# Layer 1's 128-column products as two 64-column tiles

## The chip, the core and the metric

The program runs on one core of one Trainium2 chip. A core has a matrix engine (TensorE, PE in the profile; its weight loads are shown apart as PEld), a vector engine (VectorE, DVE), a scalar engine (ScalarE, ACT), a general one (GpSimd, POOL), queues that issue transfers (SyncE, SP, is the one used most here), an on-chip memory of 128 partitions, and accumulators (PSUM) that TensorE writes and ACT and DVE read. The metric is the device time of one execution in microseconds (us); lower is better.

## What is computed

Two attention layers on an image of 128 rows x 256 positions x 256 channels, each after a group normalisation and with a residual sum. Layer 1 is the one that matters here:

```python
qkv = x2 @ w_in.T + b_in                       # x2: rows x 256 x 256
q, k, v = jnp.split(qkv, 3, axis=-1)
...
scores = jnp.einsum('bhid,bhjd->bhij', q, k) / jnp.sqrt(D)     # 4 heads of D = 64
keep = jnp.abs(i - j) <= band                                  # band = 16
scores = jnp.where(keep, scores, -jnp.inf)
attn = jax.nn.softmax(scores, axis=-1)
out = jnp.einsum('bhij,bhjd->bhid', attn, v)
...
y = out @ w_out.T + b_out
```

and then `x = x + y`. Everything is in 32-bit floats. Layer 0 is of the same build with 8 heads of 32, full attention, and a gate.

## The kernel before

Layer 0 runs over the 128 rows first, writes its result to memory, and gathers the statistics of the second normalisation. Layer 1 then runs over pairs of rows, 64 of them. In layer 1 the order of all engines and of SP is written out by hand (a manual schedule), so every engine does its instructions in the order of the program text.

The loop (i from 0 to 62) does in this order on TensorE: the scores of rows 2i and 2i+1 (tile `1sim`, line 1076, tiles of 64 rows x 64 columns); the weighted values of pair i-1 (`1av`, line 1117, 64 x 64) and their sums of weights (`1zs`, line 1129, 64 x 32); then the "stretch": the q and k products of pair i+1 and the output product of pair i-2 (`p1q`, `p1k`, `p1o`, all recorded at line 577); then the values of the next pair (`p1v`, line 1055, 128 rows x 64 columns, two column halves side by side).

A q, k or output product of a pair of rows is a 256 x 256 matrix times 2 x 256 columns. Class `Summed` does it with seven 128 x 128 products instead of eight, from sums of quarters of the weights and of rows (tiles `1ts`, `1att`, made on POOL). The seven go in the order 2, 1, 5, 6, 7, 4, 3, and at each number the three streams q, k, output take turns (`in_turn`). After each product its accumulator is read (`take`): q and k by ACT (lines 675, 677) or DVE (684, 690, 694), the output always by DVE (671 and the same three). The next product of the same stream waits for that. Each product is handed to TensorE by one helper, which cuts it into column tiles of a given width:

```python
def in_columns(out, lhsT, rhs, width, **flags):
    for c0 in range(0, P, width):
        cols = slice(c0, c0 + width)
        nc.tensor.matmul(out[cols], lhsT=lhsT[:, cols], rhs=rhs, **flags)
```

Layer 0 uses it with a width of 32 (`B`). In layer 1 the width is 128 (`P`): in `Summed.WIDTH`, and in `project`, the output product of the last six rows, which have no stretch left (`1po`). The names are P = 128, D1 = 64, B = 32.

Beside the stretch run these chains. DVE makes the reciprocals of the sums (`1z` to `1rz`, lines 1141 and 1154), in three parts between its takes; SP sends them out to memory and back, spread over partitions (`rz_far`, `1near`, lines 1162 and 1166); DVE multiplies (`1at`, line 1186), which frees the accumulator of `1av` for the next pair. In the tail the same spreading is done by a product (`1near`, line 1177, 128 x 128). A 32-bit product shows as two records (passes) in the profile, each with its weight load.

Of the kernel before, what the change touches and what calls it, by code (L numbers as in the profile page):

```python
# [15 lines left out]
P = 128  # L16
# [5 lines left out]
H1, D1 = 4, 64  # L22
# [17 lines left out]
def conv_preact_kernel(  # L40
# [35 lines left out]
    def proj_bank(name):  # L76
        return bank("proj", name)
# [67 lines left out]
    w_out_t = const.tile([P, 2, C], F32, name="w_out_t")  # L145
# [427 lines left out]
# [6 lines that stand above are left out]
    class Seven:  # L579

        WIDTH = B

# [9 lines left out]
        def product(self, n, two=None, first=False):  # L592
# [7 lines left out]
            if not self.by_token:  # L600
                in_columns(out, weights, moving, self.WIDTH, start=first, **flags)
                return
            for t2 in range(2):
                cols = slice(t2 * P, (t2 + 1) * P)
                in_columns(out[:, cols], moving[:, cols], weights, self.WIDTH, start=first and t2 == 0, **flags)

# [47 lines left out]

    class Summed(Seven):

        WIDTH = P

# [50 lines left out]
    def one_by_one(w, at, name, done, width):  # L711

        ps = proj_bank(name)
        done(ps)
        for m in range(2):
            for kt in range(2):
                in_columns(
                    ps[:, m, :], w[:, kt, m * P : (m + 1) * P], at[:, kt, :], width,
                    start=(kt == 0), stop=(kt == 1),
                )  # L720
                yield
# [10 lines left out]
    with ExitStack() as both:  # L732
# [20 lines left out]
        with ExitStack() as lay0:  # L753
            row = lay0.enter_context(tc.tile_pool(name="row0", bufs=2))
            att = lay0.enter_context(tc.tile_pool(name="att0", bufs=2))
            st, hd, outs = {}, {}, {}
# [224 lines left out]
        with ExitStack() as lay:  # L981
# [3 lines left out]
            st, hd, outs = {s: {} for s in range(S)}, {}, {}  # L985
# [38 lines left out]
            def project(s):  # L1024

                if s < 0:
                    return iter(())
                return one_by_one(w_out_t, st[s]["at"], f"1po{s}", lambda ps: st[s].update(po=ps), P)

            ats, ats_t, outputs, last_ots = {}, {}, {}, {}  # L1030

# [221 lines left out]
            with tc.manual_schedule(engines={  # L1253
# [12 lines left out]
                for i in range(last):  # L1266
                    s = 2 * i
# [22 lines left out]
                def all_of(s):  # L1290
                    for _ in project(s):
                        pass
# [240 lines left out]
```

## Time and profile before

| | |
|---|---|
| median of 3 runs | 3150.04 us (3149.86 to 3153.88) |
| the profiled execution: its time, and its span from the first to the last instruction | 3153.9 us, 3152.1 us |
| layer 1's loop and tail | from about 2071 us to the end |
| TensorE busy from 2071 to 3110 us | 1034.31 of 1039.00 us |
| DVE, ACT, POOL busy in the same stretch | 667.78, 553.72, 740.75 us |
| p1q, p1k, p1o: records, mean | 896, 896, 854; about 380 ns |
| p1v: records, mean | 4096; 274 ns |

How to read it: "128*64" behind a tile's name is the tile of the array (rows*columns) that a product uses, "128x256" is what it writes. The mean of a matmul record runs from its start to its modelled end, and passes overlap, so the step from one start to the next is the measure of what a product costs TensorE, not the mean.

### The profile page before, as it was taken

How to read it: one execution, taken by the hardware profiler on the slowest of the kernel's cores; microseconds unless marked ns; L12 is line 12 of the kernel's file. 1: busy time of each engine (PE TensorE's matmuls, PEld its weight loads, DVE VectorE, ACT ScalarE, POOL GpSimd, SP SyncE). 2: the span in 40 equal slices, each digit the busy share in tenths (PEclk: the TensorE clock that was granted, in tenths of full speed). 3: DMA queues.
4: the chain of work that ended last, by engine and by line, in shares of the span. 5: the costliest groups of instructions: out<-in, count | busy, mean ns of one | idle time of the engine just before them, and what ended most of it. 6: DMA issues, size and time to landing. Idle time of an engine off the chain costs nothing.

```text
span 3152.1 us, 128861 instructions
## 1 busy us (share of the span) xinstructions
PE 3075.5 (98%) x57467; PEld 2114.1 (67%) x57467; DVE 2544.5 (81%) x4140; ACT 1870.0 (59%) x4064; POOL 1622.5 (51%) x1651
## 2 busy tenths in 40 slices
PE   6889999999999999999999999999999999999997
PEld 4556666666666666665666666568888888888886
DVE  4669999999999999999999999956666666666665
ACT  4666666666666666666666666645555555555553
POOL 3034444444444444444444544357777777776774
PEclk9989999999999999999999999999999999999999
DMA  9941111111111111111111111114444444444443
GB/s 374 424 121 43 43 43 36 43 36 43 36 39 40 40 40 36 43 36 43 36 42 37 36 43 36 36 35 98 93 103 96 102 96 97 103 99 100 93 99 70
DMA packets 357266, 245.08 MB, mean 78 GB/s; under 512 B 276072, under 2 KB 342112, under 8 KB 350560
## 3 DMA queue, kind: packets, MB, share of 16 engines
q1 hardware_dynamic: 355808, 234.39, 27.3%
q8 instruction: 453, 7.42, 1.0%
q0 software_dynamic: 752, 2.36, 0.2%
q14 instruction: 109, 0.89, 0.1%
q10 hardware_dynamic: 144, 0.00, 0.0%
HBM read 169.09 MB, written 67.62 MB: 75 GB/s over the span
## 4 chain that ended last, share of the span: by engine, by line
PE 91%; DMA 5%; DVE 2%; ACT 1%; issue 0%; POOL 0%; SPq 0%; DVEq 0%; POOLq 0%; ACTq 0%
PE sim L794 8%; PE po L577 7%; PE p1v L1055 7%; PE bv L826 7%; PE av L826 7%; PE p1q L577 6%; PE p1o L577 6%; PE pv L577 6%; PE pq L577 6%; PE p1k L577 6%; PE pk L577 5%; PE pg L577 5%; DMA pr<-in_L_conv_pair_repr_dram 4%; PE zs L840 4%; PE 1sim L1076 3%; PE 1av L1117 3%
## 5 line engine op out<-in xcount | busy, mean ns | idle before, releaser
L807 ACT ACTIVATE ex<-sim 128x512 f32<-128x512 f32 x1024 | 547.6, 605 | 422.2 <-PE sim L794 422.2
L816 DVE TENSOR_TENSOR both<-ex 128x512 f32<-128x512 f32 x512 | 487.8, 991 | 71.2 <-ACT ex L807 71.0
L856 DVE RECIPROCAL d<-d 128x512 f32<-128x512 f32 x128 | 429.2, 3353 | 4.4
L618 POOL TENSOR_TENSOR v<-v,twovg 128x256 f32<-128x256 f32 x64 | 78.3, 1223 | 544.4 <-ACT twovg L637 544.4
L577 PE MATMUL po<-at,out_sb 128*32 128x256 f32 x4096 | 291.5, 380 | 4.1 <-DVE at L874 4.1
L794 PE MATMUL sim<-q,k 32*64 32x256 f32 x8192 | 288.4, 387 | 1.2 <-ACT ex L807 1.2
L826 PE MATMUL bv<-bias_sb,v 128*32 128x256 f32 x4096 | 244.5, 379 | 0.7 <-DVE t L871 0.7
L826 PE MATMUL av<-ex,v 128*32 128x256 f32 x4096 | 244.5, 379 | 0.0
L1086 POOL TENSOR_TENSOR 1p<-1ex,seen 128x768 f32<-128x768 f32 x127 | 231.0, 1819 | 13.9 <-ACT 1ex L1084 13.9
L1055 PE MATMUL p1v<-w_in_t,1xn 128*64 128x128 f32 x4096 | 237.7, 274 | 0.3 <-POOL place L990 0.3
L794 PEld LDWEIGHTS sim<-q,k 32*64 32x64 f32 x8192 | 152.1, 131 | 126.9 <-issue 79.3
L1055 PEld LDWEIGHTS p1v<-w_in_t,1xn 128*64 128x64 f32 x4096 | 222.3, 137 | 21.5 <-PE p1k L577 20.2
L677 ACT ACTIVATE 1q<-p1q,bqk 128x256 f32<-128x256 f32 x192 | 91.1, 474 | 244.1 <-PE p1q L577 244.1
L1186 DVE TENSOR_TENSOR 1at<-1av,1near 128x512 f32<-128x512 f32 x128 | 82.5, 686 | 151.5 <-DMA 1near<-rz_far 129.0
L618 POOL TENSOR_TENSOR q<-q,twoqk 128x256 f32<-128x256 f32 x64 | 52.0, 812 | 292.4 <-ACT twoqk L637 292.4
L826 PEld LDWEIGHTS bv<-bias_sb,v 128*32 128x32 f32 x4096 | 133.2, 110 | 88.7 <-issue 1.1
L826 PEld LDWEIGHTS av<-ex,v 128*32 128x32 f32 x4096 | 133.2, 110 | 87.9 <-issue 0.4
L577 PEld LDWEIGHTS po<-at,out_sb 128*32 128x32 f32 x4096 | 131.0, 110 | 70.9 <-issue 4.5
L1093 POOL TENSOR_TENSOR 1zp<-1p 128x512 f32<-128x512 f32 x127 | 161.9, 1275 | 10.0
L568 POOL TENSOR_TENSOR 1ts<-1xn 128x256 f32<-128x256 f32 x64 | 47.0, 734 | 232.9 <-ACT 1xn L1016 232.9
L775 DVE TENSOR_SCALAR xn<-xt,mean,rstd 128x256 f32<-128x256 f32 x256 | 160.4, 666 | 0.0
L1062 ACT COPY 1v<-p1v 128x512 f32<-128x512 f32 x128 | 75.1, 587 | 135.1 <-PE p1v L1055 131.7
(300 smaller groups left out, 7687.6 us busy)
## 6 DMA issues: line engine op xcount, KB each, us to landing
pr<-in_L_conv_pair_repr_dram SPq DMA_DIRECT2D x32, 1024.0 KB
xs<-in_x_dram SPq DMA_DIRECT2D x16, 2048.0 KB
x<-o SPq DMA_DIRECT2D x64, 512.0 KB
yg<-x SPq DMA_DIRECT2D x64, 512.0 KB
out_dram<-1o SPq DMA_DIRECT2D x256, 128.0 KB
xg<-in_x_dram SPq DMA_DIRECT2D x252, 128.0 KB
1near<-rz_far SPq DMA_DIRECT2D x124, 256.0 KB
rz_far<-1rz SPq DMA_DIRECT2D x124, 4.0 KB
```

The lines of the kernel that those rows point to most:

```text
L577: nc.tensor.matmul(out[cols], lhsT=lhsT[:, cols], rhs=rhs, **flags)
L618: nc.gpsimd.tensor_tensor(self.to[:, 0], self.to[:, 0], two, ALU.add)
L775: nc.vector.tensor_scalar(xns[i][:, 2 * r + half, :], xt[:, half, :], mean0[:, half : half + 1], rstd0[:, half : half + 1], op0=ALU.subtra ...
L794: nc.tensor.matmul(sims[j][KB * c : KB * (c + 1), kt, :], lhsT=k[p0 : p0 + D0, 2 * r + half, k0 : k0 + KB], rhs=q[p0 : p0 + D0, 2 * r + ha ...
L807: nc.scalar.activation(ex[:, j], sims[j], AF.Exp, scale=1.0 / math.sqrt(D0))
L816: nc.vector.tensor_tensor(both[:, j : j + 2], ex[:, j : j + 2, 0, :], ex[:, j : j + 2, 1, :], ALU.add)
L826: nc.tensor.matmul(to[D0 * j : D0 * (j + 1), half, :], lhsT=v[:, 2 * r + half, c0 : c0 + D0], rhs=weights(4 * half + j, kt), start=(kt == ...
L840: nc.tensor.matmul(zs[D0 * j : D0 * (j + 1), half, :], lhsT=ones[:, 0:D0], rhs=both[:, j, :], start=True, stop=True,)
L856: nc.vector.reciprocal(d, d)
L1055: nc.tensor.matmul(ps[KB * half : KB * (half + 1), b, :], lhsT=xns[i][:, 2 * r + kt, KB * b : KB * (b + 1)], rhs=w_in_t[:, kt, 2 * C + P * ...
L1086: engine.tensor_tensor(p.rearrange("p j (r c) -> p (j r) c", c=WROW)[:, :, 0 : 2 * WSTEP] .rearrange("p r (t c) -> p r t c", c=WSTEP)[:, : ...
L1093: engine.tensor_tensor(zp, p[:, :, 0:R], p[:, :, R : 2 * R], ALU.add)
```

## The change

Two widths go from 128 to 64 columns. Every q, k and output product of layer 1, and the output products of the last six rows, are then issued as two products of 64 columns each on the two column halves of the array, with the same moving operand, into the two halves of the accumulator's partitions. Nothing else is edited.

```diff
     class Summed(Seven):
 
-        WIDTH = P
+        WIDTH = D1
...
             def project(s):
 
                 if s < 0:
                     return iter(())
-                return one_by_one(w_out_t, st[s]["at"], f"1po{s}", lambda ps: st[s].update(po=ps), P)
+                return one_by_one(w_out_t, st[s]["at"], f"1po{s}", lambda ps: st[s].update(po=ps), D1)
```

## The prediction

> **What bounds the kernel now.** I read the page first (busy time, the slices, the chain of waits), then the timeline of TensorE and of its weight loads in one iteration of layer 1's loop, then who waited for whom. From the page:
>
> ```profile
> PE 3075.5 (98%) x57467; PEld 2114.1 (67%) x57467; DVE 2544.5 (81%) x4140; ACT 1870.0 (59%) x4064; POOL 1622.5 (51%) x1651
> PE   6889999999999999999999999999999999999997
> PEclk9989999999999999999999999999999999999999
> PE 91%; DMA 5%; DVE 2%; ACT 1%; issue 0%; POOL 0%; SPq 0%; DVEq 0%; POOLq 0%; ACTq 0%
> ```
>
> TensorE is the bound, at full clock, and the chain that ended last lies on it for 91% of the span. Layer 1 is the part from about 2071 us. Its loop runs 63 times, usually in 16.37 us (start of the values p1v to start of the next: 2599.88 to 2616.25), so only a change in TensorE's spacing, or in what stops TensorE, can move the end. One iteration in the timeline of TensorE (columns: start us, us, engine, line, operation, tiles, tile shape, count):
>
> ```profile
> 2599.88 3.71 PE L1055 MATMUL p1v<-w_in_t,1xn 128*64 128x128 f32 x64
> 2604.96 1.41 PE L1117 MATMUL 1av<-1p,1v 64*64 64x80 f32 x63
> 2606.31 0.66 PE L1129 MATMUL 1zs<-1zp,place 64*32 64x256 f32 x16
> 2606.90 0.70 PE L577 MATMUL p1q<-1xn,w_in_t 128*128 128x256 f32 x2
> 2607.44 0.59 PE L577 MATMUL p1k<-1xn,w_in_t 128*128 128x256 f32 x2
> 2607.87 0.59 PE L577 MATMUL p1o<-1at,w_out_t 128*128 128x256 f32 x2
> ...
> 2611.32 0.59 PE L577 MATMUL p1k<-1ts,sums_1k 128*128 128x256 f32 x2
> 2611.75 0.64 PE L577 MATMUL p1o<-1att,sums_1o 128*128 128x256 f32 x2
> 2612.23 0.59 PE L577 MATMUL p1q<-1ts,sums_1q 128*128 128x256 f32 x2
> 2612.66 0.59 PE L577 MATMUL p1k<-1ts,sums_1k 128*128 128x256 f32 x2
> 2613.09 0.64 PE L577 MATMUL p1o<-1att,sums_1o 128*128 128x256 f32 x2
> 2613.57 0.59 PE L577 MATMUL p1q<-1ts,w_in_t 128*128 128x256 f32 x2
> ...
> 2615.72 0.59 PE L577 MATMUL p1o<-1at,sums_1o 128*128 128x256 f32 x2
> 2616.25 0.33 PE L1055 MATMUL p1v<-w_in_t,1xn 128*64 128x128 f32 x2
> ```
>
> Each product is two records (two passes), so the usual 0.43 from start to start is 0.216 us a pass; the durations 0.59 overlap. The reader is to see the four places where the step is longer than 0.43: p1q to p1k 0.54, two p1o to p1q 0.48, and p1o to p1v 0.53. These are all that a tile shape can change here.
>
> **What the Trainium skill says.** TensorEngine Tiling (Array Packing), Key Properties: a change of tiling mode drains TensorE, and different tiles work in parallel. The trace agrees: from the last pass's start plus its 0.216 us, p1v starts 0.093 us late (2615.941 + 0.216 to 2616.250, the records to the ns), p1q after zs 0.09, while stages of one shape follow each other with no gap (in layer 0, products bv to av, both 128*32: 32 passes in 1.73 us, four tiles together every 0.216). TensorE: Matmul & The Clock Gate, LDWEIGHTS: a load lasts its columns / 1.2 ns, so 107 ns for 128 columns, 53 for 64. The trace shows the part that isn't hidden after a drain: p1q's first step is 0.320 instead of 0.216 (+0.104), p1v's first step 0.160 instead of 0.109 (+0.051). Same page, the paragraph on step 1 (LDWEIGHTS): loads are pulled ahead of running matmuls. Here they are issued one pass ahead, except where a wait holds them.
>
> **The change part by part.**
>
> 1. The rate of the products. Each 128-column product becomes two 64-column ones side by side. No run here has 128*64 with 256 elements moving, so I bound it: below by layer 0's helper of the same line, four 128*32 tiles of 256 elements every 0.216 us, the same as the full tile, so no cost; above by the values, pairs of 128*64 with 128 moving at 0.109 us, which doubled is 0.218: 42 steps of 2 ns, 0.1 us per iteration. I take 0. Weight loads go from 42 to 84 per iteration; two loads of a pair start 6 ns apart and the first values pair shows both exposed by only 0.051 together, so they run at once.
>
> 2. p1o to p1v (and in the first stretch p1v to p1q): now one shape. The drain of 0.093 and the exposed load of 0.051 go: 0.144 x 63 = 9.1 us. What is late next there is the values' matmul rate itself: ACT's 1v copies and the scores wait for it, not the reverse (ACT 1v waited 131.7 us for p1v).
>
> 3. zs to p1q: still a change of shape (64*32 to 128*64), so the drain stays, but the exposed load is 64 columns: 0.104 - 0.051 = 0.053.
>
> 4. The two p1o stalls, 0.044 and 0.043. The weight load of p1o (2611.69, of the product that starts at 2611.75) waits for DVE's take of the product before, then for a second wait instruction of 0.076 us; from 2611.69 it needs 0.107 and has 0.06. With 64 columns it needs 0.053. But the first take (L671 at 2611.09) starts where DVE's reciprocal ends, a chain fixed by zs, not by the products. So part 3's 0.053 brings the product forward and the shorter load just follows: after this stall the gain is 0.053 in all, not 0.097. The second take is fixed by p1o's own end (DVE idle 0.40 before it), so there the stall of 0.043 goes, with some 3 ns to spare. Other loads that wait for ACT or DVE (p1q, p1o) have 0.01 to 0.03 us to spare now; they get 0.053 more.
>
> 5. New waits. Set side by side, the two programs have the same order on every engine, but many of ACT's and DVE's takes (four ACT and nine DVE per iteration) now wait for two semaphores: PE's, and that of an older piece of work on ACT or DVE, long done. On ACT, and for p1o on DVE, the older one is waited for first, by an instruction of its own that runs before PE is done: 0. For DVE's takes of q and k PE comes first: at most one instruction of 0.05 us (L1154's: 50 ns) after PE's end. Queued behind it are the takes of k and o, and their next products on PE. Mostly DVE is still in the operation before, which hides it; uncovered it costs up to 0.05 at two places, 0.1 per iteration. I take 0.
>
> Sum per iteration: 0.144 + 0.053 + 0.043 = 0.24 us, from 16.37 to 16.13. Over the loop (61 iterations have p1o): 63 x 0.197 + 61 x 0.043 = 15.0 us. The first stretch gains 0.2.
>
> 6. What takes some of it back. In 14 of 63 iterations 1av starts 0.06 to 0.58 us later than usual, because it waits for DVE's 1at, and this for the transfer:
>
> ```profile
> DVE 1at L1186 <- DMA 1near<-rz_far: 127.3, 53, 3.7
> POOL 1att L568 <- DVE 1at L1186: 28.0, 26, 1.8
> ```
>
> The chain zs, reciprocals, two transfers (6.3 to 8.4 us from the last reciprocal to 1at), 1at, 1av has a length that the change leaves alone: in those iterations the gain is 0. Four more have less than 0.07 us in hand (1at's end to 1av 0.15 to 0.21 us, where 0.145 is the least seen); the next has 0.36. Loss: 14 x 0.24 + about 0.8 = 4.2 us.
>
> 7. The tail. There the output product alternates with the 128*128 product 1near, of one shape until now. Three new changes of shape, 0.093 + 0.05 each, about 0.4 us; half of it may lie beside DVE's reciprocals. Taken in full.
>
> 15.0 + 0.2 - 4.2 - 0.4 = 10.6 us. The profiled execution (span 3152.1, its time 3153.9) would go to 3143.3; it was the longest of the runs shown, and I take the same gain off the median: 3150.04 - 10.6 = 3139.5.
>
> **Rivals.**
>
> The waits keep more. If the new DVE waits show (0.1 us per iteration, 6 us) or the transfers are late in twice as many iterations (4 us more), 4 to 6 us are left: about 3145.5. For it: the slack of many loads is only hundredths of a us. Against: every one of them is given 0.053.
>
> More than forecast. Where the transfers' lateness came from a coincidence with loads and stores that the shorter loop shifts, nothing is lost in part 6, and the first p1o stall goes too: 15.2 + 61 x 0.044 = 17.5, about 3133.
>
> The change doesn't do what it says: the 0.093 before p1v isn't a drain but a wait (the profile names p1k as its releaser, with 0.33 us of idle weight loads). Then only parts 3 and 4 are left, 15.2 - 9.1 - 2.4 for the late iterations = 3.7, about 3146. Against: p1k had ended 0.36 us before, and three different changes of shape show the same 0.09.
>
> Slower: the halves don't run together where the first of them is held by a semaphore. Nearly every product begins with a held load. If the second half only follows in the next pass, a product costs three passes for two, 0.216 more; it decides from 49 of the loop's 1309 products (10.6 / 0.216), and for all of them gives 3139.5 + 283 = 3422. Against: layer 0's 128*32 products also begin with held loads, and their four tiles start within 0.02 us.
>
> **How the numbers follow.** Forecast 0.55, own range 3135 to 3143; waits keep more 0.13; more than forecast 0.12; no drain 0.10; slower 0.10. The range 3132 to 3147 takes in all but the slower case and the edges. 0.2%, about what a measurement of this kernel can tell from no change, is 6.3 us: faster means below 3143.7. That is the forecast, the larger gain and some 0.05 of the two smaller gains: 0.72; within 0.18; slower 0.10.
>
> **What would show it.** Right: p1v starting 0.216 us after the last p1o pass with no step over 0.11 among its first pairs; p1q to p1k 0.48; one p1o step of 0.48 instead of two; the usual iteration 16.13; 1av late in some 16 to 20 iterations. Wrong: pairs spaced over 0.22, the 0.53 step before p1v still there, new gaps after DVE's takes L684, L690 or L694, or 1av late in most iterations.

## The result, and the profile after

| | before | changed |
|---|---|---|
| median | 3152.24 us (3149.86 to 3155.4, 8 runs) | 3143.48 us (3141.82 to 3144.71, 8 runs) |
| ratio to before, from all runs | | 0.9971, 95% interval 0.9961 to 0.9982 |
| profiled execution: time, span | 3153.9, 3152.1 us | 3144.71, 3142.9 us |
| usual iteration (median), from p1v to p1v | 16.371 us | 16.175 us |
| loop, first p1v to last p1v | 1042.36 us | 1032.08 us |

The change gained 8.8 us in the medians (0.28%); the forecast was 10.6. The whole gain of the profiled pair lies in the loop: 10.28 us there. Outside it the span lost 1.1 us: 0.15 in the tail's products and 0.9 after the last of them, a part that took 13.5 us before, 14.4 here and 13.9 in another profile of the changed kernel. From the page of the changed kernel, its busy times, its instruction queue (packets, MB, share) and its chain:

```profile
PE 3062.3 (97%) x60161; PEld 2030.7 (65%) x60161; DVE 2542.5 (81%) x4140; ACT 1869.8 (59%) x4064; POOL 1623.3 (52%) x1651
q8 instruction: 474, 7.77, 1.1%
PE 91%; DMA 5%; DVE 2%; ACT 1%; issue 0%; POOL 0%; SPq 0%; DVEq 0%; POOLq 0%; ACTq 0%
```

TensorE has 2694 more records (one more for each pass of a split product) and is still the bound: DVE, ACT and POOL are as busy as before, and the chain has the same shares. TensorE's own busy time shows 13 us less, but since its records overlap, the spacing is what to read. A usual iteration in the timeline of TensorE:

```profile
2611.32 3.69 PE L1055 MATMUL p1v<-w_in_t,1xn 128*64 128x128 f32 x64
...
2617.71 0.66 PE L1129 MATMUL 1zs<-1zp,place 64*32 64x256 f32 x16
2618.30 0.65 PE L577 MATMUL p1q<-1xn,w_in_t 128*64 128x256 f32 x4
2618.79 0.60 PE L577 MATMUL p1k<-1xn,w_in_t 128*64 128x256 f32 x4
...
2620.51 0.60 PE L577 MATMUL p1o<-1at,w_out_t 128*64 128x256 f32 x4
2620.95 0.65 PE L577 MATMUL p1q<-1ts,sums_1q 128*64 128x256 f32 x4
2621.39 0.63 PE L577 MATMUL p1k<-1ts,sums_1k 128*64 128x256 f32 x4
...
2623.12 0.65 PE L577 MATMUL p1o<-1att,sums_1o 128*64 128x256 f32 x4
2623.58 0.63 PE L577 MATMUL p1q<-1ts,sums_1q 128*64 128x256 f32 x4
2624.01 0.63 PE L577 MATMUL p1k<-1ts,sums_1k 128*64 128x256 f32 x4
2624.44 0.65 PE L577 MATMUL p1o<-1att,sums_1o 128*64 128x256 f32 x4
2624.90 0.63 PE L577 MATMUL p1q<-1ts,w_in_t 128*64 128x256 f32 x4
...
2627.06 0.63 PE L577 MATMUL p1o<-1at,sums_1o 128*64 128x256 f32 x4
2627.49 3.69 PE L1055 MATMUL p1v<-w_in_t,1xn 128*64 128x128 f32 x64
```

A product is four records now, two passes of two halves side by side, and its step is still 0.432. The reader is to see four things. The last p1o to p1v is 0.43: the step of 0.53 is gone, and with it the drain, the 0.093 us by which the first product of a new tile shape started late. The first p1q to p1k is 0.49 instead of 0.54. But both of the long p1o steps are still there, at 0.46 instead of 0.48; the forecast had one of them at nothing. And the p1q of 2620.95 takes 0.44: a small stall that the kernel before didn't have.

In the table below each entry is the median over the loop of the step beyond 0.432, in thousandths of a us, from the starts of single records. The products bear the number of their order (2, 1, 5, 6, 7, 4, 3) and the stream; "3o" is the step from the last p1o to p1v, and p1v is that whole stage, from its first start to the scores'. An "exposed" weight load, below, is one that no running product hides.

| | 2q | 5q | 6k | 6o | 7k | 7o | 3o | p1v, us |
|---|---|---|---|---|---|---|---|---|
| before | 104 | 0 | 0 | 43 | 0 | 42 | 93 | 3.644 |
| changed | 51 | 16 | 4 | 21 | 4 | 21 | 0 | 3.623 |

With 11 from 1av and zs these differences make up the 0.196.

### The profile page after: what moved, and what is told of

Same layout as the page of the kernel before. It is cut to its first block, busy times and chain, and to the rows that moved or that the text cites. A ratio compares the mean times of both kernels' runs of the same rounds, so it can differ in the third digit from the quotient of the medians.

```text
span 3142.9 us, 135072 instructions
## 1 busy us (share of the span) xinstructions
PE 3062.3 (97%) x60161; PEld 2030.7 (65%) x60161; DVE 2542.5 (81%) x4140; ACT 1869.8 (59%) x4064; POOL 1623.3 (52%) x1651
## 4 chain that ended last, share of the span: by engine, by line
PE 91%; DMA 5%; DVE 2%; ACT 1%; issue 0%; POOL 0%; SPq 0%; DVEq 0%; POOLq 0%; ACTq 0%
PE sim L794 8%; PE po L577 7%; PE av L826 7%; PE bv L826 7%; PE p1v L1055 7%; PE p1q L577 6%; PE p1o L577 6%; PE p1k L577 6%; PE pv L577 6%; PE pq L577 6%; PE pk L577 5%; PE pg L577 5%; DMA pr<-in_L_conv_pair_repr_dram 4%; PE zs L840 4%; PE 1sim L1076 3%; PE 1av L1117 3%
## 5 line engine op out<-in xcount | busy, mean ns | idle before, releaser
L1055 PEld LDWEIGHTS p1v<-w_in_t,1xn 128*64 128x64 f32 x4096 | 231.6, 137 | 6.0 <-POOL place L990 0.6
L334 DVE BATCH_NORM_STATS2 stats<-xs 128x6 f32<-128x128 f32 x512 | 100.3, 277 | 65.1 <-DMA xs<-in_x_dram 65.1
```

The source lines that it names most:

```text
L1055: nc.tensor.matmul(ps[KB * half : KB * (half + 1), b, :], lhsT=xns[i][:, 2 * r + kt, KB * b : KB * (b + 1)], rhs=w_in_t[:, kt, 2 * C + P * ...
```

## The experiments

Ten kernels ran in three groups, each compared with runs of the kernel before in its group (medians 3151.65 to 3151.76 us; 3152.24 beside the changed kernel). Times are medians. The table gives what the loop of each profile showed; "late 1av" counts the iterations in which 1av starts later than usual and what those iterations lost, "other" is what was lost beyond the usual iteration in any other way.

| kernel | median | ratio to before, 95% | usual iteration | late 1av | other | loop |
|---|---|---|---|---|---|---|
| before | | | 16.371 | 13: 3.9 us | 1.1 us | 1042.36 |
| changed | 3143.48 | 0.9971 (0.9961 to 0.9982) | 16.175 | 14: 4.0 | 3.1 | 1032.08 |
| changed, once more | 3142.93 | 0.9972 (0.9962 to 0.9983) | 16.178 | 14: 3.2 | 2.8 | 1031.16 |
| e1 only product 3 split | 3151.01 | 0.9996 (0.9988 to 1.0005) | 16.371 | 6: 1.6 | 0.8 | 1039.39 |
| e2 product 5 whole again | 3157.45 | 1.0018 (1.0011 to 1.0025) | 16.459 | 10: 2.9 | 0.7 | 1046.00 |
| e3 32 columns | 3150.27 | 0.9996 (0.9987 to 1.0004) | 16.342 | 3: 1.4 | 0.8 | 1037.81 |
| e4 order of sums | 3137.28 | 0.9953 (0.994 to 0.9967) | 16.146 | 4: 1.6 | 3.1 | 1027.67 |
| e5 before, no transfers | 3147.46 | 0.9986 (0.9979 to 0.9992) | 16.367 | 0 | 0.1 | 1037.28 |
| e6 changed, no transfers | 3137.13 | 0.9953 (0.994 to 0.9967) | 16.175 | 0 | 2.2 | 1027.07 |
| e7 sums whole | 3138.39 | 0.9955 (0.9942 to 0.9969) | 16.153 | 14: 4.7 | 2.7 | 1030.96 |
| e8 e4 and e7 | 3135.56 | 0.9946 (0.9933 to 0.996) | 16.125 | 5: 1.8 | 2.7 | 1026.13 |
| e10 one shape throughout | 3195.42 | 1.0136 (1.012 to 1.0151) | | | | 1089.99 |

### Is it the change of shape? (e1, e2, e3)

e1, from the kernel before, splits only the last product of the stretch, so that p1v follows a product of its own shape and the change of shape lies three products earlier:

```diff
-                in_columns(out, weights, moving, self.WIDTH, start=first, **flags)
+                in_columns(out, weights, moving, D1 if self.WIDTH == P and n == 3 else self.WIDTH, start=first, **flags)
```

> Only the last of the seven products (number 3) is in 64-column tiles, the other six and the tail are as before. If a change of tile shape costs a drain and an exposed weight load wherever it stands: p1v follows the last p1o pass in 0.216 us, but the same 0.09 + 0.05 us appears inside the stretch, at the first p1q product of number 3; usual iteration 16.37 us as before, time within 0.1% of before. If the 0.093 us ahead of p1v is a wait of its own (for p1k or for an accumulator): no gap inside the stretch or the gap still ahead of p1v; in the first case 16.23 us and 9 us less than before.

The end of the stretch in its timeline of TensorE:

```profile
2628.06 0.59 PE L577 MATMUL p1o<-1att,w_out_t 128*128 128x256 f32 x2
2628.58 0.65 PE L577 MATMUL p1q<-1xn,sums_1q 128*64 128x256 f32 x4
2629.06 0.60 PE L577 MATMUL p1k<-1xn,sums_1k 128*64 128x256 f32 x4
2629.49 0.60 PE L577 MATMUL p1o<-1at,sums_1o 128*64 128x256 f32 x4
2629.93 0.28 PE L1055 MATMUL p1v<-w_in_t,1xn 128*64 128x128 f32 x2
```

The gap has left p1v (0.43 or 0.44 from p1o) and stands where the shape changes now: p1o to p1q 0.52 (0.092 beyond), then p1q to p1k 0.48 (0.051 beyond, the exposed load of 64 columns). The usual iteration is unchanged to the ns. So the 0.093 belongs to the change of shape, not to p1k or to p1v, and the rival "no drain" falls.

e2 is the changed kernel with product 5 in whole tiles again, which puts two more changes of shape into each stretch:

```diff
+                in_columns(out, weights, moving, P if self.WIDTH == D1 and n == 5 else self.WIDTH, start=first, **flags)
```

> All products in 64-column tiles except number 5, which keeps 128. If changes of shape are what costs: two more per iteration, 0.093 + 0.107 us into number 5 and 0.093 + 0.051 out of it, so the usual iteration is 16.17 + 0.34 = 16.51 us and the time some 63 x 0.34 = 21 us above the changed kernel, about 3165 us. If the drain costs nothing where products follow each other in one stretch: 16.17 us and about 3143 us.

```profile
2625.05 0.60 PE L577 MATMUL p1o<-1at,w_out_t 128*64 128x256 f32 x4
2625.58 0.70 PE L577 MATMUL p1q<-1ts,sums_1q 128*128 128x256 f32 x2
2626.11 0.59 PE L577 MATMUL p1k<-1ts,sums_1k 128*128 128x256 f32 x2
2626.54 0.59 PE L577 MATMUL p1o<-1att,sums_1o 128*128 128x256 f32 x2
2627.07 0.65 PE L577 MATMUL p1q<-1ts,sums_1q 128*64 128x256 f32 x4
2627.55 0.60 PE L577 MATMUL p1k<-1ts,sums_1k 128*64 128x256 f32 x4
```

In this timeline of TensorE the steps into the wide product are 0.53 and 0.53 (drain 0.100, load of 128 columns 0.104), and those out of it 0.53 and 0.48 (0.093 and 0.051). That is 0.348; 0.06 came back, since the small stalls at 5q, 6o and 7o vanish or shrink. Net 0.284 an iteration, and 14 us in the median against the changed kernel: two changes of shape cost more than the whole change gained.

e3 is the changed kernel with 32-column tiles in the stretch and the tail (`WIDTH = B`, and `B` in `project`).

> The products of layer 1 in four 32-column tiles, layer 0's shape. Shape theory: the gap ahead of p1v is back (0.093 + 0.051), p1q's first step after zs is exposed by 27 ns only; usual iteration about 16.17 + 0.14 - 0.02 = 16.29 us, plus or minus 0.04 for the held loads of p1o, and the time 3150 us, 0.1 to 0.2% above the changed kernel and about that of before. If narrow tiles were the gain by themselves (shorter loads): below 16.17 us and below 3143 us.

```profile
2611.72 0.64 PE L577 MATMUL p1o<-1at,sums_1o 128*32 128x256 f32 x8
2612.29 3.71 PE L1055 MATMUL p1v<-w_in_t,1xn 128*64 128x128 f32 x64
```

In its timeline p1o to p1v is 0.57 (0.140 beyond), so splitting as such does not help: the gap returns as soon as the tile differs from that of the values, even if both use all columns of the array in a step. The exposed load after zs fell to 0.024, which continues the row 0.104, 0.051. Three new stalls (1o 28, 6k 36, 7k 36) took the place of those at 6o and 7o. What is left is 0.029 an iteration, and the median can't be told from before. Splitting by itself gained next to nothing here; what counts is the shape of the neighbour.

### Why did the p1o stalls remain? (e4, e7, e8)

Weight loads around the second p1o stall, changed kernel, in the timeline of the loads (in brackets: idle before, and what ended it):

```profile
2623.79 0.39 PEld L577 LDWEIGHTS p1k<-1ts,sums_1k 128*64 128x64 f32 x4
2624.41 0.23 PEld L577 LDWEIGHTS p1o<-1att,sums_1o 128*64 128x64 f32 x4 [0.23 <-issue]
```

The load of this p1o is held twice: by DVE's take and by POOL's sum `1att`. With two waits, the one for DVE stands as an instruction of its own ahead of the load (it starts at 2624.338 and takes 0.051, and the load starts 0.076 after it does); the load itself waits for POOL, which is long done. e4 lets POOL form the third sum of rows before the second, so that product 6's wait for POOL covers product 7 as well:

```diff
         engine.tensor_tensor(t[:, 0], x[:, 2], x[:, 0], ALU.subtract)
-        engine.tensor_tensor(t[:, 1], x[:, 3], t[:, 0], ALU.subtract)
         engine.tensor_tensor(t[:, 2], x[:, 3], x[:, 2], ALU.subtract)
+        engine.tensor_tensor(t[:, 1], x[:, 3], t[:, 0], ALU.subtract)
```

> The changed kernel with the third row sum made before the second, so that p1o's product number 7 needs no second wait (for GpSimd). If the second wait instruction (0.076 us) is what leaves p1o stalled: the 26 ns stall at number 7 goes, that at number 6 stays, usual iteration 16.145 us, time 1 to 2 us below the changed kernel (hardly more than the measurement tells). If the stall comes from DVE's take alone: it stays, and nothing changes.

The same load in e4:

```profile
2618.62 0.35 PEld L577 LDWEIGHTS p1k<-1ts,sums_1k 128*64 128x64 f32 x3
2619.14 0.26 PEld L577 LDWEIGHTS p1o<-1att,sums_1o 128*64 128x64 f32 x4 [0.17 <-DVE mid1o L671]
```

The wait instruction is gone: the load itself now waits for DVE's take, and for nothing else, after 0.17 idle instead of 0.23, and the step of 7o is 0.432. So what remained of the second stall hung on there being two waits. The usual iteration fell by 0.029, 1.8 us over the loop. The median fell by 6, more than the steps explain. In the profile the loop is 4.4 us shorter than the changed kernel's: 2.4 of that is fewer late 1av (4 instead of 14). Most of the rest of the difference in spans lies ahead of layer 1, which began at 2064.8 us here and at 2067.7 there. Layer 0 uses the edited helper too, but that is not it: from the first scores of layer 0 to its last output product both took 1855.40 us. The difference stands before those first scores (203.35 us here, 206.19 there), in a start that the edit doesn't touch and that ranges from 203.4 to 206.4 among all profiles. Why fewer transfers were late in this kernel is not shown.

e7 shortens the chain to which the forecast tied the first p1o stall: the sums zs are formed over all 128 rows in four products instead of eight of 64 rows, and DVE's add of the halves (`1z`) goes.

```diff
-                    for half in range(2):
-                        for j in range(2):
...
+                    for j in range(2):
+                        nc.tensor.matmul(
+                            zs[strip(2 * j + r), 0, 0, :], lhsT=place, rhs=zps[r][:, j, :],
+                            start=True, stop=True,
+                        )
...
-                nc.vector.tensor_tensor(z, zs[:, 1, 0, :], z, ALU.add)
```

> The changed kernel with the sums of weights (1zs) as four products of 128 rows by 32 columns instead of eight of 64 by 32, which sums both halves of the keys at once, so that DVE's addition 1z goes. TensorE's time is the same (four tiles at once, two passes of 0.216 us; still a change of shape on both sides). The chain from zs to the transfers is 0.42 us shorter. If late transfers are what is left to gain: most of the late 1av starts go, 3 to 4 us below the changed kernel, about 3139 us, usual iteration 16.17 us or less. If they are not on the path: same time as the changed kernel.

The stage of zs fell from 0.592 to 0.569, the whole of the 0.022 by which the usual iteration fell; the stalls stayed (5q 17, 6o 22, 7o 22), and so did the 14 late 1av. In one iteration DVE's reciprocal now ends 4.71 us after zs begins, and the take after it starts only at 4.76, 0.417 after the last pass of its p1o began: that p1o holds it, not the chain from zs. The median came out 5.1 us below the changed kernel, about as expected, but not for the reason expected. In the profiles the loop gave 1.1 of it; 2.1 lie in the tail, where the edit applies as well (from the last record of p1v to the last of 1po 25.32 us in the changed kernel, 23.25 here), and 2.0 are an earlier start of layer 1. e8 has both edits.

> The kernel of the whole sums with the third row sum made before the second as well. If both add up: 16.12 to 16.15 us per usual iteration and about 3137 us. If the row sums' order does nothing: as with the whole sums alone.

Its usual iteration is 16.125, the two gains added (0.050 of 0.051), and its tail is e7's (23.25). With 3135.56 us it is the best kernel of the study, 7.9 us below the changed one.

### Do the late transfers keep some of the gain? (e5, e6)

In both kernels the transfers of the reciprocals (`by_transfer`) are left out of the loop, and `1at` is multiplied by a constant tile of 1/64; the reciprocals are still formed, and the weights of the loop's pairs are then not normalised.

```diff
-                near = att.tile([P, 2, 2, R], F32, tag="near", name=f"1near{i}", bufs=1)
+                near = near_const if i < S // 2 - 2 else att.tile([P, 2, 2, R], F32, tag="near", name=f"1near{i}", bufs=1)
...
-                            by_transfer(i - 1)
+                            pass
```

> The kernel before with the reciprocals' way through memory left out in the loop: the division takes a constant tile, so 1at waits for no transfer (the output is not the reference's for all but the last four rows). If late transfers cost what the trace shows (13 or 14 iterations, 3.9 us): 4 to 5 us below before, about 3147 us, no late 1av.

> The same taken out of the changed kernel. If the late transfers swallowed part of the gain, as predicted (4.2 us): the difference to the same kernel in 128-column tiles is the full 63 x 0.20 = 12 to 13 us, about 3134 us. If they took nothing: the difference is the 9 us seen with transfers, about 3138 us.

Without transfers no 1av is late. From e5 to e6 the change gains 10.3 us in the median, and 10.21 in the loop of the profiles; with transfers it is 8.8 and 10.28. The medians leave up to 1.5 us to the transfers, within their intervals; the loops leave nothing. Who waited for whom in the changed kernel (us in total, times, longest; before it was 127.3, 53, 3.7):

```profile
DVE 1at L1186 <- DMA 1near<-rz_far: 122.7, 53, 3.5
```

DVE waits as often as before, only a little less long. The pair shows something else as well: e6 loses 2.2 us in other places where e5 loses 0.1, so that loss is not the transfers' doing.

### What if nothing changes shape? (e9, e10)

e9 is the changed kernel once more, as a measure of the scatter.

> The changed kernel itself, on the same chip as the next run: 3143 us, 0.3% below before, usual iteration 16.17 us.

It gave 3142.93, the same steps, and 0.9 us less in the loop. e10 is e8 with the stretch, the values and zs all in 128*32 tiles:

```diff
-        WIDTH = D1
+        WIDTH = B
...
+                            for c in range(0, KB, B):
+                                nc.tensor.matmul(
+                                    ps[KB * half + c : KB * half + c + B, b, :],
+                                    lhsT=xns[i][:, 2 * r + kt, KB * b + c : KB * b + c + B],
```

> The kernel with whole sums and the other order of row sums (16.125 us, 3135.6 us), and now the products and the values in tiles of 128 rows by 32 columns, the shape that the whole sums have. An iteration then changes its shape twice instead of three times. Shape theory: p1q follows zs in 0.216 us a pass (0.093 + 0.051 us less), the values keep their rate (four tiles of 128 elements every 0.109 us), the held loads of p1o cost some 0.03 us more as in the run with four tiles: usual iteration about 16.01 us, and some 7 us less, about 3129 us. If the larger number of instructions costs more than the drain: 16.1 us or more, or late instruction fetches, and no gain.

It was 52 us slower than the changed kernel and 60 slower than e8, though every step that the idea was about came out: zs 0.456, p1q's first step and p1o to p1v 0.432. Its timeline of TensorE shows what went wrong:

```profile
2606.08 0.88 PE L1077 MATMUL 1sim<-1q,1k 64*64 64x96 f32 x28
2607.78 0.96 PE L1077 MATMUL 1sim<-1q,1k 64*64 64x96 f32 x34 [0.83 <-issue]
...
2609.97 0.64 PE L1128 MATMUL 1zs<-1zp,place 128*32 128x256 f32 x8
2610.43 0.61 PE L577 MATMUL p1q<-1xn,w_in_t 128*32 128x256 f32 x8
2610.86 0.61 PE L577 MATMUL p1k<-1xn,w_in_t 128*32 128x256 f32 x8
2611.29 0.59 PE L577 MATMUL p1o<-1at,w_out_t 128*32 128x256 f32 x3
2612.18 0.41 PE L577 MATMUL p1o<-1at,w_out_t 128*32 128x256 f32 x3 [0.29 <-issue]
```

TensorE stops in the middle of the scores, and again in the middle of one product of eight records, and what ended its idle time is "issue": nothing that the profile shows. The page gives the records, the instruction queue's transfers and the chain:

```profile
PE 3075.8 (96%) x69133; PEld 1986.7 (62%) x69133; DVE 2516.8 (79%) x4076; ACT 1871.7 (59%) x4064; POOL 1628.5 (51%) x1651
q8 instruction: 544, 8.91, 1.2%
PE 92%; DMA 4%; issue 2%; DVE 1%; ACT 1%; POOL 1%; SPq 0%; DVEq 0%; ACTq 0%; POOLq 0%
```

Each packet is 16 KB (8.91 MB / 544). TensorE's passes and loads together are 254 a packet here (2 x 69133 / 544) and in the changed kernel (2 x 60161 / 474), so I take this queue for TensorE's own. In layer 1 one comes every 5.1 us, where the changed kernel has one every 7.1 and the kernel before every 8.4. All 54 gaps above 0.5 us end little more than a us after the end of such a fetch (eight in ten within 1.26 to 1.52), and together they last some 57 us, where the loop is 64 longer than e8's. So I read them as TensorE waiting for its instructions; no run takes the fetches away. The kernel has some 27 products' records a us where it isn't stopped, each with a load; e3, with 23, shows a single gap above 0.35 us.

## Why the prediction was right, and where it was not

The direction, the mechanism of the main part and the size of the gain to within 1.8 us held. The time itself was forecast as 3139.5, with a range of 3135 to 3143, and came out just above that range: 4.0 us more, of which 2.2 are the kernel before, whose first three runs had a median of 3150.04 and all eight 3152.24. Set beside each other, per usual iteration:

| term | forecast, us | measured, us |
|---|---|---|
| part 1, rate of the products | 0 | 0 |
| part 2, drain before p1v | 0.093 | 0.093 |
| part 2, exposed load at p1v | 0.051 | 0.021 |
| part 3, and the first p1o stall of part 4, less 5q | 0.053 | 0.055 |
| part 4, second p1o stall | 0.043 | 0.017 |
| 1av and zs | 0 | 0.011 |
| sum | 0.240 | 0.196 |

Part 1: right. Two 64-column halves with 256 elements take 0.432 a product, as one whole tile did, and the rival "slower" had no product on its side: where the first half's load is held, the second follows 0.036 us later, not a pass later.

Part 2: the drain went to the ns, as e1 and e2 show from both sides; the Trainium skill's sentence in TensorEngine Tiling (Array Packing), Key Properties, that a change of tiling mode drains TensorE, holds here for a change of the columns alone, 128*128 to 128*64. The exposed load was mis-sized: 0.021 of 0.051 was gained. The reason is a lag that the forecast didn't have. Where a pair's first load has a wait of its own and a wait instruction ahead of it, the second load follows 0.036 us later (p1q of product 5: loads at 2604.738 and 2604.774; p1o of product 6: 2606.922 and 2606.958), while behind a single wait it follows after 0.006. From there on the second half of the array runs up to 0.036 behind the first, through all products of one shape and through p1v (2611.317 and 2611.353); after the change of shape at zs the two start 0.007 apart again. I read the 0.030 that p1v didn't give as this lag, come due at its end. This is read from the starts of the records; in e1, where no split product is held twice, p1v gained the full 0.051 (3.593).

Parts 3 and 4, first stall: the number was right, the reason wrong. The forecast tied DVE's take to the end of its reciprocal. In the changed kernel, in DVE's timeline:

```profile
2605.33 0.94 DVE L1154 RECIPROCAL 1rz<-1z 128x128 f32<-128x128 f32 x1
2606.32 0.48 DVE L671 SCALAR_TENSOR_TENSOR 1o<-p1o,bo_v,yg 128x256 f32<-128x256 f32 x1
```

the reciprocal ends at 2606.27 and the take starts 0.05 later. What it waits for is the second half of its own p1o: it starts 0.415 after that half's last pass began, as the take of the next p1o does, and as both did before, where reciprocal and p1o ended together to 0.01. Of the 0.053 that the product was to come forward, 5q took 0.016 and the lag 0.036, so the take stands where it stood (4.78 us after the start of zs, before and after), and p1o's load as well (5.38). From there the load of 64 columns gives its 0.054.

Second stall: this is the step that failed in part 4. By the forecast's own reckoning, with both halves ending together, the take would have come 0.054 earlier and the stall would have gone with the forecast's 3 ns to spare. The second half lags, so the take and the load come only 0.02 earlier, and 0.025 of the 0.042 stays (7k 4, 7o 21). e4 shows the other way out: with one wait less, the load is early enough in spite of the lag.

Part 5 was taken at 0, with up to 0.05 at two places; it shows at one, for 0.016. DVE's takes in the changed kernel and, in the second fence, before:

```profile
2603.70 0.48 DVE L671 SCALAR_TENSOR_TENSOR 1o<-p1o,bo_v,yg 128x256 f32<-128x256 f32 x1
2604.20 0.42 DVE L684 TENSOR_TENSOR 1q<-p1q,1q 128x256 f32<-128x256 f32 x1
```

```profile
2608.50 0.49 DVE L671 SCALAR_TENSOR_TENSOR 1o<-p1o,bo_v,yg 128x256 f32<-128x256 f32 x1
2608.93 0.42 DVE L684 TENSOR_TENSOR 1q<-p1q,1q 128x256 f32<-128x256 f32 x1
```

L684 starts 0.50 after L671 instead of 0.43. The wait for PE is an instruction of its own now, as the list of the line's instructions in the changed kernel shows (ns: least, median, most; then first and last start):

```profile
L684 DVEq EVENT_SEMAPHORE  x189: 21/21/21, 2073.1 to 3093.1; - x189
```

The load of the next p1q waits for this take and comes 0.03 later after zs than before (3.197 us instead of 3.165, medians), though the products ahead of it come 0.054 earlier; that is the stall at 5q. This is read from the trace; no run takes DVE's wait away by itself.

Part 6 is the term that failed most: it gave 4.2 us back to late transfers, and the pair of profiles gave back 0.1 (13 late 1av with 3.9 us before, 14 with 4.0 after). The forecast held each lateness fixed from zs on, iteration by iteration. It isn't. What the late ones share is a fetch of instructions by TensorE: of the 26 whose way from the last reciprocal to 1at was over 7.4 us in the kernel before, 23 ended 2.0 to 2.5 us after such a 16 KB fetch, and all 16 in the changed kernel did; the others took 6.6 us (median). In the shorter loop other iterations were hit, which fits transfers that have moved against the fetches. It is in part what the rival "more than forecast" supposed, only that nothing was gained by it. Among the profiles with transfers the late 1av cost between 1.4 and 4.7 us, which no step of mine could have told. That the fetches cause the lateness is argued from this coincidence; no run takes them away.

What no part had: TensorE lost 2 us more inside its stages (3.1 instead of 1.1). In the changed kernel's profile two thirds of that are four gaps of 0.34 to 0.74 us in the middle of 1av, each ending 1.27 to 1.44 us after a fetch, as in e10; the profile of e9 has four more, of 0.36 to 0.55. But e3 has more fetches and loses only 0.8, so the count of instructions alone doesn't explain it. It comes with kernels whose stretch and values have one shape (2.2 to 3.1 in all six profiles of that kind); why, stays open.

Part 7 was too dear: 0.15 instead of 0.4 in the tail.

So the sum was 15.2 - 4.2 - 0.4 = 10.6; measured in the profiles, 63 x 0.196 = 12.3 less 0.1, 2.0 and 0.15, and less 0.9 after the tail, which I count as scatter. Usual steps that gave 2.9 too little and lateness that cost 4.1 too little nearly cancelled: that the total came so close is luck. (In the rival "more than forecast" the sum as written, 15.2 + 61 x 0.044, is 17.9; the 17.5 there has the tail's 0.4 taken off.)

## What to carry to other kernels

Where TensorE is the bound, list the tile shapes in the order in which it meets them: each change of shape cost a drain (0.09 us) and a weight load that nothing hid (up to 0.10) here. Giving neighbours one shape removed the drain, and the load as far as no lag of one half took its place (0.021 of 0.051 here, all of it in e1); splitting without that gained 0.03 us an iteration (e3). Count what the split adds to the stream of instructions before going on with it: the finest split removed the most drains and lost 52 us. And a forecast that spends hundredths of a us of slack must ask which instruction of a doubled set is held, and by how many waits.

## What the runs showed of the hardware that was not expected

It seems that TensorE can run out of instructions in unrolled code. The Trainium skill, Runtime: NRT & Kernel Launch, Instruction fetch mechanics, says that an engine's instructions are fetched in blocks of 16 KiB (256 instructions) while earlier ones run, and that the cost of this is mostly hidden. The size agrees with the 16 KB packets, and the number with the 254 passes and loads in each; if the gaps are waits for instructions, the hiding holds at a fetch every 7.1 us only nearly (gaps up to 0.74 us in four places), holds at one every 5.6 us in e3, and fails at one every 5.1 us, with gaps of 0.5 to 2.3 us.

An exposed weight load after a change of shape was 0.104, 0.051 and 0.024 us for 128, 64 and 32 columns (e2's wide product, the changed kernel, e3). The Trainium skill, TensorE: Matmul & The Clock Gate, LDWEIGHTS, gives columns / 1.2 ns, so 107, 53 and 27: these runs agree to 3 ns.
